# A cross-attention block: projection products 1 and 7 in quarters, softmax inverses read back from DRAM, the second score tile lowered on VectorE

## The chip, the cores and the metric

One NeuronCore of a Trainium2 chip runs the whole program. The metric is device time in microseconds for one execution. Five engines run their own instruction lists side by side, each in order: TensorE (matmuls, with weight loads shown apart), VectorE, ScalarE, GpSimd, and SyncE, which here only issues DMAs. Semaphores join them.

## The reference

```python
xq  = _ada_ln(x_q,  t_vec, Wss_q,  bss_q)      # x: (16, 1024, 512), layer norm, scaled and shifted per batch
xkv = _ada_ln(x_kv, t_vec, Wss_kv, bss_kv)     # context: (16, 64, 512)
q   = (xq @ Wq + bq).reshape(B, Lq, nh, dh)    # 16 heads of 32
kv  = (xkv @ Wkv + bkv).reshape(B, Lkv, 2, nh, dh)
scores = jnp.einsum('bqhd,bkhd->bhqk', q, k) / jnp.sqrt(jnp.float32(dh))
attn = jax.nn.softmax(scores, axis=-1)
out  = jnp.einsum('bhqk,bkhd->bqhd', attn, v).reshape(B, Lq, H)
return x_q + (out @ Wp + bp)
```

All of it is float32. Nearly all the arithmetic lies in the two 512x512 products over 16,384 rows: the query projection and the output projection.

## The kernel before

**Tiling.** The rows are cut into NB = 32 blocks of 512, two per batch element. Keys and values of all batch elements are made on the way in and stay in SBUF. A block i then passes through these stages, each a small helper:

- `load_x` (1 MB), `q_stats` (two VectorE instructions for each of four 128-row tiles), `q_scale` (five small ScalarE and four small GpSimd operations), `hidden` (ScalarE normalises), `turn` and `move` (VectorE transposes 32x32 pieces, 16 DMAs put them in place), `scale_features` (ScalarE), `feature_sums` (GpSimd).
- `query_product(i, 1..7)`: the 512-row block and the weights are each cut into 2x2 halves, and seven products with sums around them take the place of eight. A product is four matmuls of 128x128 weights and 256 columns. Each float32 matmul shows as two records in the trace, so a product has eight. Query products 1 and 7 are cut once more by the same scheme: `feature_quarters` (GpSimd, three additions), `quarter_products` (seven matmuls of 128 columns, the first four and the last three apart), `quarter_copies` (ScalarE) and `quarter_adds` (VectorE, three additions in PSUM between the two parts). `query_out` (ScalarE) and `query_added` (VectorE) take the results out.
- `score_products(i, z)` for z = 0, 1, the two halves of 32 keys. It fills two pairs of PSUM banks, and there are just two such pairs (`ps_s`, two buffers), so the next user of a pair has to wait for all its readers. `maximum(i, z, e)` (VectorE) and `copied(i, z, e)` (ScalarE, into `s_tiles`) read them. `maxima` joins the maxima and spreads them over a tile `mb`.
- `subtract` for both z (GpSimd, 2048 elements per partition each), `weights` (exp on ScalarE), `swapped` and `again` (the first half of the weights is rearranged so that `mix` can contract over 64 rows), `total` (GpSimd adds both halves), `row_total` (VectorE sums over the keys).
- `inverse_rows`: VectorE's reciprocal, a write to DRAM, four reads of 8 KB back. `spread_rows` (VectorE transposes a broadcast of them over a whole tile `vb`). `mix(i)` uses the same two pairs of score banks; `divided(i, (e,))` multiplies them by `vb` into `ot` and so frees them.
- `row_sum` (GpSimd, four sums over halves of `ot`), `biased` and `output_seed` (ScalarE puts the bias, or a copy of the other bank, into a PSUM bank), `product(i, 1..7)` for the output projection in the same seven-product scheme, `added` (VectorE adds a bank to the residual tile), and an output DMA after `added` 3 and 4.

**Order.** Nothing is scheduled by a library: the calls at the end of the function, from line 1296 on, give every engine its list, in that order. Lines 1296 to 1757 are the way in, lines 1759 to 1875 the steady loop over i = 3 to 29, the rest the way out. A round of the loop works on several blocks at once: scores of i, statistics of i + 4, query products of n = i + 1, mixing and projection of a = i - 1 and b = i - 2. All DMAs of the loop are issued by SyncE, in order, and an issue that waits for a semaphore holds up those behind it.

**Helpers that are there, but not called.** The file holds `inner_weight_sums`, `inner_biased`, `inner_quarters`, `inner_products`, `inner_copies`, `inner_adds`, `reciprocal_rows`, `read_rows`, `q_stats_two` and `q_square_mean`; `lowered` is called for block 30 alone.

Of the kernel before, what the change touches and what calls it, by code (L numbers as in the profile page):

```python
# [20 lines left out]
def cross_attention_block(  # L21
# [1646 lines left out]
    query_product(3, 6)  # L1668
    turn(4, (3,))
    load_x(6)  # L1670
    row_total(1)
    added(0, 2)
    query_product(3, 2)
    move(4, ks=(0,))
    again(1, 0)
    inverse_rows(1)
    weight_sums()
    move(4, ks=(1,))
    move(4, ks=(2,))
    biased(0, 3)  # L1680
    maximum(2, 1, 1)
    maximum(2, 1, 0)
    maxima(2)
    product(0, 7)
    move(4, ks=(3,))
    row_sums(0, 1)
    product(0, 6)
    again(1, 1)
    hidden(5, (0,))
    subtract(2, zs=(0,))  # L1690
    added(0, 7)
    product(0, 4)
    hidden(5, (1,))
    added(0, 6)
    q_stats(6, (0,))
    query_out(3, 2)
    query_out(3, 6)
    product(0, 5)
    q_stats(6, (1,))
    q_stats(6, (2,))  # L1700
    q_stats(6, (3,))
    added(0, 5)
    feature_sums(3, nc.gpsimd, (3,))
    spread_rows(1)
    copied(2, 1, 1)
    copied(2, 1, 0)
    mix(1)
    product(0, 3)
    added(0, 4)
    subtract(2, zs=(1,))  # L1710
    weights(2, 0)
    added(0, 3)
    divided(1)
    row_sums(1, 0)
    turn(5, (0,))
    turn(5, (1,))
    turn(5, (2,))
    hidden(5, (3,))
    query_product(3, 7)
    query_out(3, 7)  # L1720
    query_product(3, 5)
    query_added(3, 5)
    weights(2, 1)
    query_product(3, 4)
    biased(1, 2)
    product(1, 1)
    scale_features(4, (2,))
    turn(5, (3,))
    load_x(7)
    added(1, 1)  # L1730
    scale_features(4, (0,))
    scale_features(4, (1,))
    scale_features(4, (3,))
    product(1, 2)
    total(2)
    feature_quarters(4, 1)
    query_product(3, 3)
    query_added(3, 4)
    swapped(2)
    added(1, 2)  # L1740
    feature_sums(4, nc.gpsimd, (0,))
    biased(1, 3)
    row_total(2)
    move(5, ks=(0,))
    row_sums(1, 1)
    query_out(3, 3)
    feature_sums(4, nc.gpsimd, (1,))
    q_scale(6)
    feature_sums(4, nc.gpsimd, (2,))
    weight_quarter_sums(7)  # L1750
# [3 lines left out]
    inverse_rows(2)  # L1754
    feature_sums(4, nc.gpsimd, (3,))
    move(5, ks=(3,))
    load_residual(2)

    for i in range(3, NB - 2):
        a, b, n, f = (i - 1, i - 2, i + 1, i + 2)  # L1760
        score_products(i, 0)
        maximum(i, 0, 0)
        quarter_products(n, 1, True)
# [26 lines left out]
        if i + 4 < NB:  # L1790
            q_stats(i + 4, (0,))
# [267 lines left out]
```

## Time and profile before

| | |
|---|---|
| median of 3 runs | 998.18 us (997.47 to 998.61) |
| the profiled execution | 996.79 us, with a span of 994.9 us |
| granted TensorE clock | 1.0 throughout |
| one round of the loop | 28.57 us |

The span runs from the first to the last instruction of the profile. Busy time counts overlapping instructions of an engine once. A line such as L1155 is that of the helper that issues the instruction, so projection products of all blocks stand under one line; the names left and right of the arrow are output and inputs. A wait is put down to the engine whose signal came last. The ends of matmuls are modelled, so their starts are what to measure with.

### The profile page before, as it was taken

What the parts mean: (1) busy time and instruction counts of PE and PEld (TensorE: products, weight loads), DVE (VectorE), ACT (ScalarE), POOL (GpSimd) and SP (SyncE); (2) the same over time, 40 slices, a digit from 0 to 9 for tenths busy, and PEclk for the clock granted to TensorE, in tenths of its full rate; (3) what the DMA queues carried; (4) which work ended last, traced back from release to release, by engine and by line L of the source; (5) the groups of instructions that cost most, each with busy time, mean ns of one, the idle gap of its engine ahead of it and who ended that gap; (6) DMA issues with size and microseconds to landing.
All of it is one profiled execution on the core that took longest, in us unless ns stands there. A gap on an engine that the chain in (4) does not pass through costs nothing.

```text
span 994.9 us, 20661 instructions
## 1 busy us (share of the span) xinstructions
PE 982.9 (99%) x7501; PEld 767.7 (77%) x7501; DVE 898.5 (90%) x1326; ACT 780.2 (78%) x1169; POOL 893.0 (90%) x695
## 2 busy tenths in 40 slices
PE   8999999999999999999999999999999999999997
PEld 7888777777777777777777778777787787777776
DVE  7687899999999999999999999999999999987995
ACT  3878868888888888888888888888888888876540
POOL 2687999999999999999999999999999999999861
PEclk9999999999999999999999999999999999999999
DMA  9765755555656555556655555565555556544323
GB/s 316 257 173 148 172 161 143 156 161 171 190 181 181 164 152 164 142 180 191 184 178 159 160 154 151 182 188 181 178 152 172 149 155 182 148 135 131 116 90 108
DMA packets 114885, 165.52 MB, mean 166 GB/s; under 512 B 34872, under 2 KB 46160, under 8 KB 112864
## 3 DMA queue, kind: packets, MB, share of 16 engines
q1 hardware_dynamic: 114400, 163.67, 55.2%
q8 instruction: 60, 0.98, 0.4%
q0 software_dynamic: 384, 0.54, 0.2%
q14 instruction: 41, 0.34, 0.1%
HBM read 79.21 MB, written 34.60 MB: 114 GB/s over the span
## 4 chain that ended last, share of the span: by engine, by line
PE 94%; POOL 1%; DMA 1%; SPq 1%; DVE 1%; issue 1%; DVEq 0%; ACT 0%; POOLq 0%
PE pp L1155 37%; PE pq L551 29%; PE pq L622 10%; PE ps L755 7%; PE po L1002 6%; PE pk_A L551 1%; PE pv_B L551 1%; PE pk_B L551 1%; PE pv_A L551 1%; DMA w_k_sb<-in_L_xcond_Wkv_dram 1%; PE pp_0b L1155 1%; POOL sum L902 0%; SPq L166 0%; SPq L143 0%; DVE m L772 0%
## 5 line engine op out<-in xcount | busy, mean ns | idle before, releaser
L814 POOL TENSOR_TENSOR s<-s,mb 128x2048 f32<-128x2048 f32 x63 | 286.1, 4563 | 16.5 <-DVE mb L801 9.2
L1155 PE MATMUL pp<-w_p_sb,ot 128*128 128x256 f32 x756 | 178.9, 380 | 0.2 <-DVE ot L981 0.2
L772 DVE TRANSPOSE_TENSOR_REDUCE m<-ps 128x32 f32<-128x1024 f32 x128 | 152.3, 1226 | 10.0 <-PE ps L755 9.7
L781 ACT COPY s<-ps 128x1024 f32<-128x1024 f32 x126 | 127.4, 1013 | 41.8 <-PE ps L755 36.9
L1155 PEld LDWEIGHTS pp<-w_p_sb,ot 128*128 128x128 f32 x756 | 141.2, 190 | 21.9 <-issue 1.9
L662 ACT ACTIVATE qt<-pq,bias_t 128x256 f32<-128x256 f32 x256 | 107.5, 474 | 52.9 <-PE pq L622 27.8
L902 POOL TENSOR_TENSOR sum<-s,p 128x2048 f32<-128x2048 f32 x30 | 136.4, 4547 | 1.6 <-ACT p L836 1.6
L1288 DVE TENSOR_TENSOR r<-pp,r 128x512 f32<-128x512 f32 x188 | 123.6, 669 | 14.2 <-ACT xt L459 6.8
L551 PE MATMUL pq<-xt,w_q_sums 128*128 128x256 f32 x512 | 123.8, 385 | 0.0
L1155 PE MATMUL pp<-WT,ot 128*128 128x256 f32 x508 | 122.0, 383 | 0.0
L551 PEld LDWEIGHTS pq<-xt,w_q_sums 128*128 128x128 f32 x512 | 95.2, 190 | 34.3 <-issue 22.6
L1155 PE MATMUL pp<-WT,s 128*128 128x256 f32 x504 | 119.6, 380 | 0.7 <-DVE r L1288 0.5
L861 ACT ACTIVATE s<-s 32x2048 f32<-32x2048 f32 x60 | 114.6, 1910 | 1.5
L1155 PEld LDWEIGHTS pp<-WT,ot 128*128 128x128 f32 x508 | 94.2, 190 | 17.8 <-issue 3.0
L1155 PEld LDWEIGHTS pp<-WT,s 128*128 128x128 f32 x504 | 91.5, 191 | 11.9 <-DVE r L1288 1.4
L344 ACT ACTIVATE x<-x,rstdq 128x512 f32<-128x512 f32 x128 | 94.8, 807 | 1.0 <-POOL rstdq L305 0.9
L459 ACT ACTIVATE xt<-xt,ss_q 128x512 f32<-128x512 f32 x124 | 93.9, 807 | 0.5 <-DMA xt<-ht 0.3
L981 DVE TENSOR_TENSOR ot<-po,vb 128x1024 f32<-128x1024 f32 x64 | 75.5, 1219 | 18.8 <-PE po L1002 17.4
L287 DVE BATCH_NORM_STATS2 bs<-x 128x6 f32<-128x512 f32 x128 | 85.3, 666 | 0.0
L510 POOL TENSOR_TENSOR xt_sums<-xt 128x512 f32<-128x512 f32 x64 | 81.2, 1268 | 1.4 <-ACT xt L459 0.9
L374 DVE STREAM_TRANSPOSE ht<-x 128x512 f32<-128x512 f32 x124 | 77.7, 679 | 4.3 <-ACT x L344 2.2
L907 DVE TRANSPOSE_TENSOR_REDUCE lt<-sum 128x64 f32<-128x2048 f32 x31 | 71.6, 2310 | 6.2 <-POOL sum L902 3.9
(221 smaller groups left out, 1957.6 us busy)
## 6 DMA issues: line engine op xcount, KB each, us to landing
x<-in_x_dram SPq DMA_DIRECT2D x32, 1024.0 KB, 5.4
r<-in_x_dram SPq DMA_DIRECT2D x32, 1024.0 KB, 5.7
out_dram<-r SPq DMA_DIRECT2D x62, 512.0 KB, 5.0
xt<-ht SPq DMA_DIRECT2D x488, 64.0 KB, 2.0
p<-s SPq DMA_DIRECT2D x60, 256.0 KB, 3.8
wss_kv<-in_L_xcond_Wss_kv_dram SPq DMA_DIRECT2D x4, 512.0 KB, 7.2
wss_q<-in_L_xcond_Wss_q_dram SPq DMA_DIRECT2D x4, 512.0 KB, 10.5
vr<-ltd SPq DMA_DIRECT2D x128, 8.0 KB, 1.8
```

Source lines behind the costliest of these rows:

```text
L344: nc.scalar.activation(dst, src, AF.Identity, bias=rstd[:, 1, j : j + 1], scale=rstd[:, 0, j : j + 1])
L459: nc.scalar.activation(xt[:, :, c, :], xt[:, :, c, :], AF.Identity, scale=ss["q"][:, c, b : b + 1], bias=ss["q"][:, NC + c, b : b + 1],)
L551: nc.tensor.matmul(out_, lhsT=lhsT, rhs=rhs, start=new and m == 0 and c == 0, stop=c == HC - 1, skip_group_check=True,)
L622: nc.tensor.matmul(qa["q", k][:, q * P : (q + 1) * P], lhsT=lhsT, rhs=rhs, start=first and q == 0, stop=True, skip_group_check=True,)
L662: nc.scalar.activation(dst, src, AF.Identity, bias=bq_t[:, o : o + 1])
L772: nc.vector.tensor_reduce(m_tiles[i][:, z, 2 * e : 2 * e + 2, :], s_banks[i, z][e].rearrange("p r (j a) -> p r j a", a=32), AX.X, ALU.max, ...
L781: nc.scalar.copy(s_tiles[i, z][:, 2 * e : 2 * e + 2, :], s_banks[i, z][e])
L814: eng.tensor_tensor(s_tiles[i, z], s_tiles[i, z], mb_tiles[i], ALU.subtract)
L861: nc.scalar.activation(s_tiles[i, 0][at + 32 : at + 64], raw_tiles[i][at : at + 32], AF.Exp, scale=SCALE)
L902: nc.gpsimd.tensor_tensor(t, s_tiles[i, 0], s_tiles[i, 1], ALU.add)
L1155: nc.tensor.matmul(to, lhsT=rows[:, c, t * P : (t + 1) * P], rhs=cols[:, c, :], start=n == 2 and (i, 2) not in seeded and t == 0 and c == ...
L1288: nc.vector.tensor_add(r, a, r)
```

## The change

Five things change. First, for blocks 2 to 28, projection products 1 and 7 are made in quarters, as query products 1 and 7 already are: `product(i, 1)` and `product(i, 7)` with their `biased` give way to `inner_biased` (two half-size copies into the bank), `inner_quarters` (three GpSimd additions), `inner_products` in two parts, `inner_copies` (ScalarE) and `inner_adds` (three VectorE additions):

```python
def inner_quarters(i, v, eng=nc.gpsimd):
    ...
    tt(t[:, 0:2], x[:, 1, 0:2, :], x[:, 0:2, 0, :], ALU.subtract)
    tt(t[:, 2], x[:, 1, 1, :], t[:, 0], ALU.subtract)
    tt(t[:, 3], x[:, 0, 1, :], t[:, 2], ALU.subtract)
def inner_adds(i, v):
    a, t, tt = acc[acc_bank(i, v)], inner_tiles[i, v], nc.vector.tensor_tensor
    both_ = a[:, P : 3 * P].rearrange("p (k n) -> p k n", k=2)
    tt(t[:, 2], a[:, 3 * P :], t[:, 0], ALU.add)
    tt(both_, both_, t[:, 2:3].to_broadcast([P, 2, P]), ALU.add)
    tt(a[:, 3 * P :], a[:, P : 2 * P], t[:, 1], ALU.add)
```

The weight sums for it are made on the way in by `inner_weight_sums(1)` and `(7)` on GpSimd. They overwrite a part of the weights and of a bias, which the new `inner_restored` puts back for blocks 29 to 31.

Second, from block 2 to block 30 the inverses are spread by DMA: `reciprocal_rows` makes the reciprocal, transposes it (64 elements per partition) and writes it to DRAM, and `read_rows` reads it back in four DMAs that each broadcast rows over 32 partitions of `vb`. `spread_rows` goes there.

```python
def reciprocal_rows(i):
    ...
    nc.vector.reciprocal(flat, flat)
    nc.vector.transpose(v.rearrange("p k a -> p (k a)"), flat)
    nc.sync.dma_start(d.rearrange("k x a -> x k a"), v)
def read_rows(i, rs=range(HPC)):
    ...
        src = src[r % 2 : r % 2 + 1].to_broadcast([32, NC, TB])
        nc.sync.dma_start(vb_tiles[i][32 * r : 32 * r + 32], src)
```

Third, for blocks 3 to 30, the second score tile isn't copied out by ScalarE and then lowered by GpSimd. `lowered(i, e)` on VectorE subtracts the maxima straight from the PSUM banks into the SBUF tile, in two instructions of 1024 elements per partition.

Fourth, for one of the four tiles of a block, from block 7 on, the statistics are made by `q_stats_two` on ScalarE (two passes of 512 elements with accumulators) and `q_square_mean` on GpSimd.

Fifth, the loop body is rotated and its order is new. The first part of a round now finishes the query products of i, mixes b and begins its projection; the part after `score_products(i, 0)` is the later one. The order of the last part of the way in and of the way out is new too. The banks of the projection are swapped for block 30, where they were swapped for 29 and 31.

```diff
-        return (2 if n in (1, 6, 5, 3) else 3) - (2 if i in (NB - 3, NB - 1) else 0)
+        return (2 if n in (1, 6, 5, 3) else 3) - (2 if i == NB - 2 else 0)
...
-            z_halves.append(bank(f"pp_{i}_0", 0))
+            z_halves.append(bank(f"pp_{i}_0", 2))
...
+    def inner_restored(v):
+        tt = nc.gpsimd.tensor_tensor
+        tt(inner_weight(v, 1, 0), inner_weight(v, 0, 0), inner_weight(v, 1, 0), ALU.subtract)
+        if v == 7:
+            tt(b_diff[:, P:], b_diff[:, P:], b_diff[:, :P], ALU.add)
...
```

The order of a round after, for i = 4 to 28 and with the conditions on i left out. Calls separated by semicolons stand on lines of their own in the file:

```python
quarter_adds(i, 7); scale_features(n, (0,)); scale_features(n, (1,)); product(i - 3, 3); mix(b)
subtract(a, zs=(0,)); scale_features(n, (3,)); quarter_products(i, 7, False); query_product(i, 5)
added(i - 3, 3); turn(f, (1,)); divided(b, (0,)); feature_quarters(n, 1); added(i - 3, 4)
weights(a, 0); inner_biased(b, 1); query_out(i, 7); inner_quarters(b, 1); divided(b, (1,))
inner_products(b, 1, True); turn(f, (2,)); weights(a, 1); query_added(i, 5); turn(f, (3,))
row_sum(b, 0); query_product(i, 4); load_x(i + 4); inner_copies(b, 1); inner_adds(b, 1)
q_stats_two(i + 3, (0,)); total(a); query_product(i, 3); query_added(i, 4); move(f, ks=(0,))
query_out(i, 3); q_stats(i + 3, (1,)); inner_products(b, 1, False); score_products(i, 0)
row_sum(b, 2); scale_features(n, (2,)); quarter_products(n, 1, True); q_stats(i + 3, (2,))
output_seed(b); q_stats(i + 3, (3,)); swapped(a); copied(i, 0, 1); quarter_copies(n, 1)
row_sum(b, 1); product(b, 2); maximum(i, 0, 0); maximum(i, 0, 1); q_square_mean(i + 3, range(1))
inner_quarters(b, 7); quarter_adds(n, 1); product(b, 6); added(b, 2); copied(i, 0, 0)
row_total(a); move(f, ks=(1,)); feature_sums(n, nc.gpsimd, (0,)); feature_sums(n, nc.gpsimd, (1,))
quarter_products(n, 1, False); q_scale(i + 3); inner_biased(b, 7); inner_products(b, 7, True)
query_seed(n); feature_sums(n, nc.gpsimd, (2,)); inner_copies(b, 7); move(f, ks=(2,)); again(a, 0)
hidden(i + 3, (3,)); score_products(i, 1); query_product(n, 2); reciprocal_rows(a); query_out(n, 2)
hidden(i + 3, (0,)); row_sum(b, 3); load_residual(a); move(f, ks=(3,)); added(b, 6)
inner_adds(b, 7); maximum(i, 1, 1); again(a, 1); hidden(i + 3, (2,)); inner_products(b, 7, False)
product(b, 5); query_product(n, 6); feature_quarters(n, 7); maximum(i, 1, 0); read_rows(a, (0, 1))
quarter_products(n, 7, True); added(b, 7); product(b, 4); query_out(n, 6); maxima(i); added(b, 5)
read_rows(a, (2, 3)); quarter_copies(n, 7); lowered(i, 1); hidden(i + 3, (1,))
feature_sums(n, nc.gpsimd, (3,)); lowered(i, 0); turn(i + 3, (0,))
```

More of the change, by code (lines that the diff above doesn't have):

```diff
@@ L1688, in cross_attention_block @@
+    inverse_rows(1)
+    again(1, 0)
+    maximum(2, 1, 1)
+    query_out(3, 2)
+    feature_sums(3, nc.gpsimd, (2,))
+    maxima(2)
+    product(0, 6)
+    added(0, 6)
+    hidden(5, (2,))
+    hidden(5, (3,))
+    scale_features(4, (0,))
+    added(0, 7)
+    scale_features(4, (1,))
+    query_product(3, 7)
+    product(0, 5)
+    added(0, 5)
     again(1, 1)
+    load_x(6)
+    copied(2, 1, 0)
+    copied(2, 1, 1)
+    query_product(3, 6)
     hidden(5, (0,))
+    query_out(3, 6)
+    product(0, 4)
@@ L1724, in cross_attention_block @@
+    product(1, 1)
+    added(0, 4)
     query_product(3, 4)
-    biased(1, 2)
-    product(1, 1)
     scale_features(4, (2,))
+    feature_sums(4, nc.gpsimd, (0,))
     turn(5, (3,))
+    query_product(3, 3)
     load_x(7)
-    added(1, 1)
[L1731 to L1739, printed above, removed]
+    query_added(3, 4)
+    product(1, 2)
+    inner_weight_sums(1)
@@ new lines, in cross_attention_block @@
+        if i >= 4:
+            move(f, ks=(3,))
+        added(b, 6)
+        if i >= 4:
+            inner_adds(b, 7)
+        maximum(i, 1, 1)
+        again(a, 1)
+        if i < NB - 3:
+            hidden(i + 3, (2,))
+        if i >= 4:
+            inner_products(b, 7, False)
+        product(b, 5)
+        query_product(n, 6)
+        feature_quarters(n, 7)
+        maximum(i, 1, 0)
+        if i >= 4:
+            read_rows(a, (0, 1))
+        quarter_products(n, 7, True)
+        added(b, 7)
@@ L1869, in cross_attention_block @@
-        load_residual(i)
-        row_sum(a, 3)
-        feature_sums(f, nc.gpsimd, (2,))
-        feature_sums(f, nc.gpsimd, (3,))
-        product(a, 7)
-        if i == NB - 3:
-            load_residual(NB - 1)
-    y, z = (NB - 2, NB - 1)
+    y, z = (NB - 2, NB - 1)
+    scale_features(31, (0,))
+    product(27, 3)
+    scale_features(31, (1,))
+    added(27, 4)
+    mix(28)
+    quarter_adds(30, 7)
+    added(27, 3)
+    divided(28, (0,))
+    divided(28, (1,))
+    subtract(29, zs=(0,))
@@ new lines, in cross_attention_block @@
+    quarter_products(30, 7, False)
+    scale_features(31, (3,))
+    inner_biased(28, 1)
+    weights(29, 0)
+    feature_quarters(31, 1)
+    query_out(30, 7)
+    query_product(30, 5)
+    query_added(30, 5)
+    weights(29, 1)
+    load_residual(NB - 1)
+    load_residual(29)
+    inner_quarters(28, 1)
+    inner_products(28, 1, True)
+    query_product(30, 4)
+    query_product(30, 3)
+    inner_copies(28, 1)
+    scale_features(31, (2,))
+    inner_adds(28, 1)
+    row_sum(28, 0)
+    total(29)
@@ L1877, in cross_attention_block @@
+    query_added(30, 4)
+    swapped(29)
+    inner_products(28, 1, False)
+    row_sum(28, 2)
+    row_sum(28, 1)
+    feature_sums(31, nc.gpsimd, (0,))
+    query_out(30, 3)
     score_products(y, 0)
+    inner_quarters(28, 7)
+    output_seed(28)
     maximum(y, 0, 0)
@@ L1920, in cross_attention_block @@
-    query_added(z, 5)
+    added(28, 2)
+    quarter_products(z, 1, False)
+    inner_biased(28, 7)
+    query_seed(z)
+    feature_sums(31, nc.gpsimd, (1,))
+    row_total(29)
+    inner_products(28, 7, True)
+    added(y - 2, 6)
+    score_products(y, 1)
+    inner_copies(28, 7)
+    inner_adds(28, 7)
+    again(y - 1, 0)
+    feature_sums(31, nc.gpsimd, (2,))
+    reciprocal_rows(29)
+    maximum(y, 1, 0)
+    query_product(z, 2)
+    query_out(z, 2)
+    inner_products(28, 7, False)
+    maximum(y, 1, 1)
@@ new lines, in cross_attention_block @@
+    query_product(z, 6)
+    maxima(y)
+    feature_quarters(z, 7)
+    quarter_products(z, 7, True)
+    again(y - 1, 1)
+    product(y - 2, 5)
+    row_sum(28, 3)
+    added(y - 2, 7)
+    query_out(z, 6)
+    quarter_copies(z, 7)
+    lowered(y, 0)
+    read_rows(29, (0, 1))
+    lowered(y, 1)
+    query_product(z, 5)
+    added(y - 2, 5)
+    read_rows(29, (2, 3))
+    quarter_adds(z, 7)
+    weights(y, 1)
+    product(y - 2, 4)
+    subtract(y, zs=(0,))
+    added(y - 2, 4)
+    inner_restored(1)
@@ L1953, in cross_attention_block @@
[L1953 to L1977 removed]
+    subtract(z, zs=(1,))
```

537 lines of the change are left out of this document (277 added, 260 removed).

## The prediction

> **What bounds the kernel now.** I read the page's first two parts and its chain, then busy time by round of the steady loop, then forms of instruction, waits, and timelines of one round.
>
> ```profile
> span 994.9 us, 20661 instructions
> PE 982.9 (99%) x7501; PEld 767.7 (77%) x7501; DVE 898.5 (90%) x1326; ACT 780.2 (78%) x1169; POOL 893.0 (90%) x695
> PE 94%; POOL 1%; DMA 1%; SPq 1%; DVE 1%; issue 1%; DVEq 0%; ACT 0%; POOLq 0%
> ```
>
> TensorE is 99% busy and 94% of the chain, but a busy share hides how near the others are. Two table answers of busy time by stretch say it: one round of the loop, with the mean of ten such rounds, then three stretches outside it (stretch, its length; busy time and instructions of TensorE, its weight loads, VectorE, ScalarE, GpSimd; granted clock, DMA share, GB/s).
>
> ```profile
> 500.00:528.57 28.57, 28.57 (x222) 22.22 (x221) 27.03 (x40) 24.07 (x36) 27.56 (x23) 1.00 0.59 174
> sum 285.70, PE 285.70 PEld 222.31 DVE 270.16 ACT 240.62 POOL 275.42; mean PE 28.57 PEld 22.23 DVE 27.02 ACT 24.06 POOL 27.54
> ...
> 120.00:160.00 40.00, 39.72 (x292) 30.38 (x291) 36.74 (x48) 30.44 (x42) 39.05 (x34) 1.00 0.53 151
> 940.00:960.00 20.00, 18.24 (x187) 12.15 (x186) 18.42 (x19) 8.54 (x11) 12.94 (x7) 1.00 0.31 109
> 980.00:994.90 14.90, 9.38 (x44) 7.86 (x42) 6.47 (x13) 0.00 (x0) 1.68 (x2) 0.98 0.39 142
> ```
>
> A round takes 28.57 us, all of it TensorE. VectorE has 1.54 us left, GpSimd 1.0, ScalarE 4.5. So TensorE work that goes is worth its time only until VectorE is full, and the change moves work onto VectorE. That is the whole question.
>
> **TensorE: what is saved.** The query products 1 and 7 already have the form that projection products 1 and 7 get. A stretch of TensorE's timeline shows both forms side by side (start, length, what; starts count, since lengths overlap).
>
> ```profile
> 500.93 1.89 PE L551 MATMUL pq<-xt_sums,w_q_sums 128*128 128x256 f32 x8
> 502.66 0.38 PE L622 MATMUL pq<-xt_sums,w_q_sums 128*128 128x128 f32 x2
> 502.88 0.83 PE L622 MATMUL pq<-t_quarters,w_p_sb 128*128 128x128 f32 x6
> 503.55 0.81 PE L1155 MATMUL pp<-w_p_sb,ot 128*128 128x256 f32 x3
> ```
>
> A whole product is 8 records in 502.66 − 500.93 = 1.73 us, 216 ns each. The first four small products are 8 records in 503.55 − 502.66 = 0.89 us, 111 ns each. Seven of them are 14 records, 1.56 us. A product saves 0.17 us, a round 0.33, and TensorE needs 28.24. 27 blocks (2 to 28) change, so the whole could give 27 × 0.33 = 8.9 us.
>
> The Trainium skill ("TensorE: Matmul & The Clock Gate", Back-to-back issue gap) speaks against this: in a stream of weight loads and matmuls it gives about 81 ns for 128 columns, against 56 for a lone one, since the load counts too. By that ratio (an estimate from the page's figures) a small record would take 111 × 81 / 56 = 161 ns and a product 2.25 us, 0.5 more than now, some 28 us over 27 blocks. The rows above are such a stream, and show 111: the trace does not agree, and the sum goes without that rule.
>
> **VectorE: what is added.** Forms with their mean, two waits, and two stretches of its timeline:
>
> ```profile
> L957 DVE STREAM_TRANSPOSE vb<-vr 128x2048 f32<-128x2048 f32 x31 | 71.3, 2301 | 0.7 <-DMA vr<-ltd 0.7
> L818 DVE TENSOR_TENSOR s<-ps,mb 128x1024 f32<-128x1024 f32 x2 | 2.4, 1220 | 0.1
> L287 DVE BATCH_NORM_STATS2 bs<-x 128x6 f32<-128x512 f32 x128 | 85.3, 666 | 0.0
> L288 DVE BATCH_NORM_AGGREGATE mvq<-bs 128x2 f32<-128x6 f32 x128 | 23.3, 182 | 4.4
> L374 DVE STREAM_TRANSPOSE ht<-x 128x512 f32<-128x512 f32 x124 | 77.7, 679 | 4.3 <-ACT x L344 2.2 <-ACT qt L662 1.0 <-DMA xt<-ht 0.8
> ...
> DVE ot L981 <- PE po L1002: 17.4, 26, 1.1
> DVE m L772 <- PE ps L755: 9.7, 28, 1.0
> ...
> 523.87 0.25 DVE L639 TENSOR_TENSOR t_quarters<-pq,t_quarters 128x128 f32<-128x128 f32 x1
> 524.16 0.43 DVE L640 TENSOR_TENSOR pq<-pq,t_quarters 128x256 f32<-128x256 f32 x1
> 524.63 0.30 DVE L641 TENSOR_TENSOR pq<-pq,t_quarters 128x128 f32<-128x128 f32 x1
> 524.84 0.68 DVE L1288 TENSOR_TENSOR r<-pp,r 128x512 f32<-128x512 f32 x1
> 525.48 2.38 DVE L772 TRANSPOSE_TENSOR_REDUCE m<-ps 128x32 f32<-128x1024 f32 x2
> ```
>
> Independent neighbours overlap by 0.09 and 0.04 here (524.63 + 0.30 against 524.84, 524.84 + 0.68 against 525.48), about 0.07; dependent ones leave 0.04 (524.16 + 0.43 against 524.63). Per round:
> - `lowered` twice, 1.22 each less 0.07: +2.30.
> - `inner_adds` twice. The trace has no such line, but `quarter_adds` has the same three forms: 524.84 − 523.87 = 0.97 each, +1.94.
> - the small transpose in `reciprocal_rows`, 64 elements. No row shows one. Between the smallest VectorE row (0.18) and the 512-element transpose (0.68); the line through 512 (0.68) and 2048 (2.30) gives 0.20, and I take that.
> - `spread_rows` gone: 2.30 less 0.07, −2.23.
> - one tile's statistics to ScalarE: 0.67 + 0.18 less an overlap, −0.81.
>
> Sum +1.40. What VectorE needs now is 27.0 to 27.5: busy 27.02, while of the 1.54 idle about 17.4/26 + 9.7/28 = 1.0 are waits for TensorE, which end when VectorE never catches up; each that ends gives back an overlap of 0.07, so I take the low end. After: 28.4 to 28.9, taken 28.4. **VectorE takes over as the bound**, 0.16 above TensorE's 28.24, and 0.17 below the old round.
>
> **What covers the rest.** GpSimd and ScalarE, by these forms; the DMAs with KB and median landing; one issue on SyncE's timeline:
>
> ```profile
> L814 POOL TENSOR_TENSOR s<-s,mb 128x2048 f32<-128x2048 f32 x63 | 286.1, 4563 | 16.5 <-DVE mb L801 9.2 <-ACT qt L662 7.2
> L598 POOL TENSOR_TENSOR t_quarters<-xt 128x256 f32<-128x256 f32 x28 | 20.5, 732 | 0.0
> L599 POOL TENSOR_TENSOR t_quarters<-xt,t_quarters 128x128 f32<-128x128 f32 x28 | 12.9, 460 | 2.2
> L781 ACT COPY s<-ps 128x1024 f32<-128x1024 f32 x126 | 127.4, 1013 | 41.8 <-PE ps L755 36.9 <-DVE m L772 3.9
> L633 ACT COPY t_quarters<-pq 128x256 f32<-128x256 f32 x56 | 21.0, 374 | 2.7 <-PE pq L622 1.8
> L1099 ACT COPY pp<-b_diff 128x512 f32<-128x512 f32 x32 | 18.8, 589 | 42.8 <-DVE r L1288 42.8
> L344 ACT ACTIVATE x<-x,rstdq 128x512 f32<-128x512 f32 x128 | 94.8, 807 | 1.0 <-POOL rstdq L305 0.9
> ...
> x<-in_x_dram SPq DMA_DIRECT2D x32, 1024.0 KB, 5.4
> p<-s SPq DMA_DIRECT2D x60, 256.0 KB, 3.8
> ltd<-lt SPq DMA_DIRECT2D x32, 32.0 KB, 1.7
> ...
> 499.52 0.59 SPq L399 DMA_DIRECT2D xt<-ht  x1
> ```
>
> GpSimd loses one subtraction (4.56) and gains two `inner_quarters` of 0.73 + 0.46 + 0.46 with gaps near 0.08 (3.6 together) and a tiny multiplication (0.2): about 26.8 of 28.4. ScalarE loses two copies (−2.03) and two bias copies (−1.18); it gains four half-size ones and two `inner_copies` (six at 0.374, +2.24) and two passes of `q_stats_two` at 0.59 to 0.81 each, with an accumulator write that no row shows (at most another small 0.3 each): +0.2 to +1.2 on 24.06. Its 4.5 us idle hide that; without them it would be added whole.
>
> The inverse now goes out and comes back as four broadcasts of 256 KB. On SyncE's queue they stand behind the write (1.7), the residual load and four moves. Between the reciprocal and the next `divided` VectorE's list holds four large additions and two transposes (0.6 each), six small additions (1.94), two maxima (2.4), the spread of the maximum (2.3, the form of `spread_rows`, and 0.3) and the two `lowered` (2.3): 12.8 us. Write 1.7, ten issues at 0.59 and a landing of 3.8 (5.4, the 1 MB load, at worst) make 11.4 to 13.0. I cost it at nothing; at worst `divided` comes 0.2 late, and then both pairs of score banks. Behind the two reads, which wait for the write to land, SyncE's queue holds the next round's outputs, its load of x and its moves. Those moves feed `scale_features` a round later, and the moves of this round are issued ahead of the reads, so nothing near waits for them. The DMA share rises from 0.59 by about 1 MB in 5, to some 0.7.
>
> All other steps are moved, not changed: product 3 and the additions of products 3 and 4 cross into the next round with their two output DMAs, `swapped` goes behind `total` by a score product, the residual load ahead of the reads, the statistics of block i+3 stand where those of i+4 stood. Each keeps its engine and length, so the sums hold; what a new order can cost is waits, below. Projection bank numbers shift for block 30 in place of 29 and 31, on the way out.
>
> The way in gains about 5 us on GpSimd (`inner_weight_sums`, ten small operations near 0.46), between 120 and 160 us, where it is busy 39.05 of 40; round 3 gives a subtraction back. Between 0 and +5; I take +0.7. The way out has 1.8 + 5.5 us of idle TensorE: a new order could win or lose 2 either way; I take 0, with the 0.33 of block 28.
>
> **Sum.** Rounds 4 to 29: 26 × (28.57 − 28.40) = 4.4; + 0.3 − 0.7 = 4.0 faster. The profiled execution took 996.79 (span 994.9 and 1.9 around it), so 992.8; the median of the three runs, 998.18, is 1.4 above it, so **994.2**.
>
> **The rivals.**
>
> *TensorE keeps the lead.* If VectorE's order closes up better than I sum (28.2), the full 8.9 comes: 989.3. For it: four more instructions that overlap. Against: a VectorE without a single wait.
>
> *A draw.* The saving is eaten by VectorE at 28.5 to 28.6, or in the way in: 996.2 to 1000.2, center 998.2. For it: the upper half of my bounds begins right there.
>
> *Slower: the ring through the score banks.* Before, ScalarE's copies freed the second pair of score banks. Now `lowered`, last but one on VectorE's list, frees it; `mix` needs that pair and `divided` needs `mix`.
>
> ```profile
> 507.45 0.39 PE L622 MATMUL pq<-t_quarters,w_q_sums 128*128 128x128 f32 x2
> 507.76 1.09 PE L1002 MATMUL po<-s,V_A 64*32 64x512 f32 x16
> 508.65 1.06 PE L1002 MATMUL po<-p,V_A 64*32 64x512 f32 x16
> 509.64 2.00 PE L551 MATMUL pq<-xt,w_q_sums 128*128 128x256 f32 x8
> 509.80 2.36 DVE L981 TENSOR_TENSOR ot<-po,vb 128x1024 f32<-128x1024 f32 x2 [0.65 <-PE po L1002]
> ```
>
> `mix` takes 509.64 − 507.76 = 1.88, and `divided` starts 0.16 later: 2.04. VectorE has two transposes (0.61 each), three small additions (0.97) and one large (0.60) between, 2.8. So TensorE may come to `mix` at most 0.7 us late, with `product(i-3, 3)`, 1.73 us, queued ahead of it. If it comes later, VectorE waits, and behind that wait stand its whole list and, through the inner products, TensorE. It decides from 0.17 us of VectorE wait a round. Half of today's 1.0 gives 28.9, 26 × 0.33 = 8.6 more, 1006.
>
> **How the numbers follow.** Forecast (faster than 996.2) 0.42; TensorE leads 0.11; draw 0.21; slower 0.26. Own range of the forecast: 991 to 996. The range for 8 in 10 leaves out the best of the second and the worse half of the last: 987.5 to 1004. Under 0.2% (2 us) a measurement of this kernel can't be told from no change. Faster 0.53, within 0.21, slower 0.26.
>
> **What would show it.** In a round after: TensorE with 0.1 to 0.3 us idle where it had none, VectorE over 28 of some 28.4; `inner_products` at 111 ns a record; `divided` with waits for `mix` under 0.2 us a round (the ring, if 0.5); no wait for the broadcasts. Wrong if the round exceeds 28.57, if the way in puts off the first round by several us, or if the broadcasts land late.

## The result, and the profile after

The changed kernel takes 1030.57 us (median of four runs, 1026.54 to 1033.39), the kernel before 998.3 beside it: a ratio of 1.0322, with an interval from 1.0284 to 1.0359. It is 32 us slower, where 4 us faster was forecast. The profiled execution took 1033.39 us, with a span of 1031.6.

The first and fourth parts of the page after: span, busy time, and the chain that ended last, by engine.

```profile
span 1031.6 us, 22024 instructions
PE 998.7 (97%) x7825; PEld 779.8 (76%) x7825; DVE 922.3 (89%) x1492; ACT 796.4 (77%) x1323; POOL 869.7 (84%) x869
DVE 40%; DMA 31%; PE 21%; issue 3%; POOL 3%; SPq 2%; ACT 1%; DVEq 0%; POOLq 0%
```

Before, TensorE held 94% of the chain and DMAs 1%. Now DMAs hold 31%, and VectorE, which starts when they land, 40%. The starts of the score products divide the span (us, read from the trace; score 4 is the first of block 4):

| | before | after | load behind the reads | way in rearranged |
|---|---|---|---|---|
| start of the first score product | 59.35 | 61.84 | 59.80 | 59.53 |
| start of score 4 | 177.92 | 182.41 | 179.86 | 178.30 |
| score 4 to score 29, 25 rounds | 713.11 | 740.38 | 711.28 | 709.65 |
| one round | 28.52 | 29.62 | 28.45 | 28.39 |
| score 29 to the end | 103.87 | 108.82 | 107.56 | 106.95 |

(The last two columns are runs told below.) Of the 36.7 us that the span grew, 27.3 are in the loop, 4.9 behind it, 2.0 in the way in and 2.5 ahead of the first score product, where both kernels hold the same instructions: there the granted clock was 0.83 from 20 to 30 us in this execution, 1.00 before, which is 1.7 of the 2.5. The 28.57 us that stands for a round of before ahead of the prediction is the width of the stretches that were asked for; by the starts of the score products it is 28.52. What a round waits for stands in the waits of after, and the landing times in its DMA issues (KB, median us to landing):

```profile
DVE ot L981 <- DMA vb<-ltd: 26.0, 22, 2.5
DVE ot L981 <- PE po L1002: 0.6, 1, 0.6
ACT xt L459 <- DMA xt<-ht: 20.7, 15, 2.9
ACT xt L459 <- DMA vb<-ltd: 17.4, 10, 2.7
...
r<-in_x_dram SPq DMA_DIRECT2D x32, 1024.0 KB, 6.5
xt<-ht SPq DMA_DIRECT2D x488, 64.0 KB, 3.3
vb<-ltd SPq DMA_DIRECT2D x116, 256.0 KB, 6.4
```

`divided` (L981) waits for the broadcasts in 22 rounds, 26.0 / 22 = 1.2 us each. That is the growth of a round. The broadcasts land in 6.4 us, where 3.8 was taken and 5.4 was the worst allowed for; the moves take 3.3 for 2.0, and `scale_features` (L459) waits for them. It reads only what the moves bring, though ten of its waits are put down to the broadcasts. One round on SyncE's timeline, then on VectorE's, and the chain through it:

```profile
517.36 0.53 SPq L938 DMA_DIRECT2D ltd<-vr  x1
517.93 0.49 SPq L126 DMA_DIRECT2D r<-in_x_dram  x1
518.48 2.41 SPq L399 DMA_DIRECT2D xt<-ht  x4
521.29 3.84 SPq L948 DMA_DIRECT2D vb<-ltd  x4
...
515.83 0.55 DVE L936 RECIPROCAL lt<-lt 128x64 f32<-128x64 f32 x1
...
528.57 0.70 DVE L374 STREAM_TRANSPOSE ht<-x 128x512 f32<-128x512 f32 x1
530.30 1.23 DVE L981 TENSOR_TENSOR ot<-po,vb 128x1024 f32<-128x1024 f32 x1 [1.03 <-DMA vb<-ltd]
...
517.93 6.88 DMA r<-in_x_dram
524.83 5.35 DMA vb<-ltd
```

VectorE's list from the reciprocal's end (516.38) to where `divided` could start (529.27) is 12.9 us long; the prediction counted 12.8. But the last broadcast lands at 524.83 + 5.35 = 530.18, 13.8 after the reciprocal, where 11.4 to 13.0 was worked out. The chain runs through the 1 MB residual load, issued between the write and the reads.

### The profile page after: what moved, and what is told of

It is laid out like the page before. It is cut to its first block, busy times and chain, and to the rows that moved or that the text cites. A ratio compares the mean times of both kernels' runs of the same rounds, so it can differ in the third digit from the quotient of the medians.

```text
span 1031.6 us, 22024 instructions
## 1 busy us (share of the span) xinstructions
PE 998.7 (97%) x7825; PEld 779.8 (76%) x7825; DVE 922.3 (89%) x1492; ACT 796.4 (77%) x1323; POOL 869.7 (84%) x869
## 4 chain that ended last, share of the span: by engine, by line
DVE 40%; DMA 31%; PE 21%; issue 3%; POOL 3%; SPq 2%; ACT 1%; DVEq 0%; POOLq 0%
DMA r<-in_x_dram 15%; DMA vb<-ltd 14%; PE pq L551 7%; DVE m L772 6%; DVE lt L907 5%; DVE ot L981 5%; DVE bs L287 4%; DVE r L1295 4%; PE pp L1155 3%; DVE ht L374 3%; DVE qt L669 3%; PE ps L755 2%; DVE pp L1271 2%; PE pk_A L551 1%; POOL s L814 1%
## 5 line engine op out<-in xcount | busy, mean ns | idle before, releaser
L814 POOL TENSOR_TENSOR s<-s,mb 128x2048 f32<-128x2048 f32 x36 | 164.1, 4563 | 23.7 <-DVE mb L801 21.5
L1155 PE MATMUL pp<-w_p_sb,ot 128*128 128x256 f32 x540 | 128.0, 380 | 1.8 <-ACT pp L1108 0.7
L459 ACT ACTIVATE xt<-xt,ss_q 128x512 f32<-128x512 f32 x124 | 94.6, 810 | 38.8 <-DMA xt<-ht 20.7
L551 PE MATMUL pq<-xt,w_q_sums 128*128 128x256 f32 x512 | 121.1, 379 | 0.0
L1155 PEld LDWEIGHTS pp<-w_p_sb,ot 128*128 128x128 f32 x540 | 98.0, 190 | 16.3 <-issue 2.7
L981 DVE TENSOR_TENSOR ot<-po,vb 128x1024 f32<-128x1024 f32 x64 | 77.7, 1220 | 31.7 <-DMA vb<-ltd 26.0
L344 ACT ACTIVATE x<-x,rstdq 128x512 f32<-128x512 f32 x128 | 103.7, 818 | 2.1 <-POOL rstdq L305 1.0
L1155 PEld LDWEIGHTS pp<-WT,s 128*128 128x128 f32 x504 | 93.5, 190 | 12.8 <-DVE r L1295 0.8
L374 DVE STREAM_TRANSPOSE ht<-x 128x512 f32<-128x512 f32 x124 | 85.9, 697 | 10.5 <-DMA xt<-ht 5.4
L781 ACT COPY s<-ps 128x1024 f32<-128x1024 f32 x72 | 72.8, 1014 | 12.0 <-PE ps L755 6.1
L551 PEld LDWEIGHTS pq<-xt,w_q_sb 128*128 128x128 f32 x288 | 52.0, 189 | 32.6 <-ACT seventh L1264 22.6
L836 ACT ACTIVATE s<-s 128x2048 f32<-128x2048 f32 x34 | 64.8, 1908 | 14.6 <-POOL s L814 11.1
L801 DVE STREAM_TRANSPOSE mb<-m 128x2048 f32<-128x2048 f32 x32 | 74.0, 2311 | 1.2
```

The lines of the kernel that those rows point to most:

```text
L344: nc.scalar.activation(dst, src, AF.Identity, bias=rstd[:, 1, j : j + 1], scale=rstd[:, 0, j : j + 1])
L374: nc.vector.transpose(ht_tiles[i][:, :, :, t, :].rearrange("p k c b -> p c k b"), x_tiles[i][:, t, :].rearrange("p (c k b) -> p c k b", c= ...
L551: nc.tensor.matmul(out_, lhsT=lhsT, rhs=rhs, start=new and m == 0 and c == 0, stop=c == HC - 1, skip_group_check=True,)
L814: eng.tensor_tensor(s_tiles[i, z], s_tiles[i, z], mb_tiles[i], ALU.subtract)
L981: nc.vector.tensor_tensor(ot[:, cs, :], po[e], vb[:, cs, :], ALU.mult)
L1155: nc.tensor.matmul(to, lhsT=rows[:, c, t * P : (t + 1) * P], rhs=cols[:, c, :], start=n == 2 and (i, 2) not in seeded and t == 0 and c == ...
```

## The experiments

**Where the reads lose their time.** In after, the fourth read is issued late, since its issue waits until the residual load has landed, eight DMAs earlier (26 such waits, 50.6 us together): the four issues above take 3.84 us. The first run issues one move ahead of the load, so that the fourth read is seven DMAs behind it, and no longer waits. The second puts the load behind the reads.

```diff
 # one move ahead
+    move(f, ks=(3,), gs=(0,))
     load_residual(a)
-    move(f, ks=(3,))
+    move(f, ks=(3,), gs=(1, 2, 3))
 # load behind the reads
-    load_residual(a)
     move(f, ks=(3,))
 ...
     read_rows(a, (2, 3))
+    load_residual(a)
```

> The changed kernel, but one of the four moves that stood behind the residual load is issued ahead of it; the load itself starts about 0.6 us later, and beside the reads as before. Theory Q (queue): in the changed kernel's trace the fourth read of a round is issued 1.9 us after the third, when the residual load has landed, which was issued exactly eight DMAs earlier; with one move between, that wait goes, the last read is issued 0.5 us after the third and lands about 1.5 us sooner, the 1.0 us of VectorE's wait for it goes, and a round falls from 29.6 to 28.6 us: about 1005. Theory B (bandwidth: the reads land late because 1 MB of residual is moved beside their 1 MB): the round stays at 29.4 to 29.6, about 1029. Theory V (VectorE is full at 28.3 us busy and its gaps make the rest): 29.6, about 1030.

> The changed kernel with the residual load issued behind the four reads of the round. Takes away the queue's wait and the traffic beside the reads at once. Q: as with one move ahead, 28.6 a round, about 1005. B: 28.5, about 1003, with the reads landing in about 4 us in place of 6.4, and clearly below the run with one move ahead. V: 29.6, about 1030.

One move ahead: 1030.43 us (1028.45 to 1031.86), ratio 1.033 (1.0313 to 1.0346). The four reads are issued in 1.76 us, yet they land no sooner (DMA issues and a wait of this run):

```profile
vb<-ltd SPq DMA_DIRECT2D x116, 256.0 KB, 7.2
DVE ot L981 <- DMA vb<-ltd: 25.3, 23, 2.3
```

The issue queue falls as a cause: only the next DMA, an output, now waits for the load (26 waits, 52.4 us). Load behind the reads: 1000.5 us (999.58 to 1001.99), ratio 1.0028 (1.0016 to 1.0041). The same rows, and a round of its busy time by stretches:

```profile
r<-in_x_dram SPq DMA_DIRECT2D x32, 1024.0 KB, 7.9
vb<-ltd SPq DMA_DIRECT2D x116, 256.0 KB, 4.8
DVE ot L981 <- DMA vb<-ltd: 2.6, 1, 2.6
...
456.88:485.32 28.44, 28.44 (x240) 22.53 (x233) 27.90 (x46) 24.58 (x42) 26.45 (x28) 1.00 0.70 198
```

The reads land in 4.8 us, the load pays (7.9) and nobody waits for it, and the round is 28.44. So 30 of the 32 us came from the place of one load. A third run asks whether one queue served in order makes the reads late, or the sharing of the DMA engines: the load keeps its place, but ScalarE issues it.

```diff
-    load_residual(a)
+    load_residual(a, nc.scalar)
```

> Edit: the changed kernel, with the residual load of the loop at its place in the list, but issued by ScalarE on its own queue in place of SyncE's. Nothing is left out. It asks why the load beside them makes the reads late. Theory O (one queue in order: the reads' packets stand behind the megabyte in each engine's ring, as one queue serves them in turn): with the load on another queue the reads land in about 4.8 us as with the load behind them, the round is 28.44 to 28.5, the time 1000 to 1003. Theory S (the 16 engines share their time whatever the queue): reads and load still run side by side, landing 6 us or more, round 29.3 to 29.7, time 1024 to 1033. In between (landing near 5.5, round 28.7 to 29.2) both have a part.

```profile
vb<-ltd SPq DMA_DIRECT2D x116, 256.0 KB, 7.3
r<-in_x_dram ACTq DMA_DIRECT2D x26, 1024.0 KB, 6.2
DVE ot L981 <- DMA vb<-ltd: 28.7, 24, 2.7
```

1030.98 us in one execution, as slow as on one queue. The order within a queue falls too. What is left, by exclusion, is that load and reads share the DMA engines, whichever queue they come from.

**Whether VectorE and TensorE were sized right.** One run brings the old spread by VectorE back into the loop (`inverse_rows`, `spread_rows`), and the four broadcasts go. Another, with the load behind the reads, goes back to whole products 1 and 7 (the weight sums, `inner_restored` and all steps of the small products go with them).

```diff
-    reciprocal_rows(a) ... read_rows(a, (0, 1)) ... read_rows(a, (2, 3))
+    inverse_rows(a)    ...                          spread_rows(a)
```

> The changed kernel with the inverses of blocks 3 to 28 spread by VectorE's transpose again, the residual load where the change put it. VectorE gets 2.2 us more and loses a small transpose: 28.3 + 2.0 = 30.3 us busy in a round. Q and B: VectorE becomes the bound, a round of 30.4 to 30.8, about 1050. If the round should fall below 29.6, the reads cost more than VectorE's transpose, and VectorE was not near its end (against V and against my sum).

```diff
-    inner_biased(b, 1) ... inner_products(b, 1, True) ... inner_products(b, 1, False)
+    biased(b, 2)       ... product(b, 1)
     # the same for product 7
```

> The run with the residual load behind the reads, and projection products 1 and 7 of all blocks whole again (the weight sums and what puts the weights back go too). TensorE then needs 28.5 us a round as before the change, VectorE 26.4. Q and B: 28.5 to 28.6 a round, bound by TensorE; the difference to the run with the residual behind is what the small products bring. If VectorE is the bound there at 28.6 or more, this run is as fast or faster. V: 28.5, since VectorE is relieved.

With the spread back, 1055.64 us and a round of 30.58, in quiet rounds 30.14 to 30.30. The price worked out, 2.23 less the 0.20 of the small transpose, put on the 28.4 predicted for VectorE makes 30.4. Whole products: 1026.33 us, a round of 29.44, where 28.5 to 28.6 was expected. The order was written for products in two parts; without the second part nothing stands between query product 3 and the scores, and the waits show it:

```profile
DVE m L772 <- PE ps L755: 41.1, 58, 3.1
PE ps L755 <- ACT qt L662: 16.4, 29, 0.6
```

So that run doesn't price the small products by themselves.

**Why the round is 28.44 and not 28.24.** With the load behind the reads TensorE has no gap in a round. But a busy stretch hides a wait. The timeline of all engines at the first score product of a round (start, length, engine, line):

```profile
463.90 0.84 ACT L662 ACTIVATE qt<-pq,bias_t 128x256 f32<-128x256 f32 x2 [0.74 <-PE pq L551]
464.46 1.45 PE L755 MATMUL ps<-qt,K_A 32*32 32x512 f32 x32
464.79 0.21 PEld L755 LDWEIGHTS ps<-qt,K_A 32*32 32x32 f32 x24 [0.18 <-ACT qt L662]
465.85 0.49 PE L622 MATMUL pq<-xt,w_q_sb 128*128 128x128 f32 x2
```

From its start to the next product it takes 465.85 - 464.46 = 1.39 us, the second score product of a round 1.07. Eight weight loads go in, those of the first of four column groups, then 24 wait for the second half of `query_out`. That is 0.31 of the 0.33 that a round saves; without it TensorE would need 28.13 where before took 28.52. Only the 0.67 us second part of the small product now stands between query product 3 and the scores, where before had a whole projection product of 1.73. The next runs try to fill the hole: by taking the column groups in another order, then by rearranging the way in as well, then by halves of query products 4 and 3.

```diff
 # scores turned (blocks 4 to 29, first score product)
-    for c in range(NC):
+    for c in (2, 3, 0, 1):
 # way in, on top of it
-    copied(2, 1, 0)  copied(2, 1, 1)  ...  subtract(2, zs=(1,))
+    lowered(2, 0)    lowered(2, 1)
+    query_out(3, 3)  score_products(3, 0)    # ahead of biased(1, 3), product(1, 7)
+    load_residual(2)                         # behind read_rows(2, (2, 3))
```

> Edit: the residual load behind the reads, as in the run before, and the first score product takes its four column groups in the order 2, 3, 0, 1 in place of 0, 1, 2, 3, in blocks 4 to 29. Nothing is left out. Open after the last runs: the round was 28.44 us and TensorE without a gap in it, where the prediction needed 28.24. Theory H (a hidden hole): the small products do save 0.33 us a round, but the first score product starts on group 0 and then stands 0.3 us inside what counts as one busy stretch, since the second half of product 3's query_out (columns 0 and 1) ends after it began; groups 2 and 3 had their last addition 0.9 us earlier. Turned round, the hole is filled with groups 2 and 3, and the round falls to what the next engine allows: TensorE 28.13, VectorE 28.2 to 28.3 by the run that gave it 2.3 us more. So 28.25 (28.13 to 28.35), 26 rounds x 0.19 = 5 less than 1000.5: 995.5 (992.5 to 998). Theory F (TensorE is full at 28.44, the score product simply takes that long): round 28.44, time 1000.5 +- 1. A third way, VectorE already bounds at 28.4: round 28.40 to 28.44, with TensorE showing a gap elsewhere.

> Edit: the run above, and three moves in the way in: block 2's second score tile lowered by VectorE from the score banks (lowered, twice) in place of two copies by ScalarE and one subtraction of 4.6 us by GpSimd; query_out(3,3) and the first score product of block 3 ahead of biased(1,3) and product(1,7); the residual load of block 2 behind its reads. Nothing is left out. Theory W (the way in lost its 2 us to GpSimd, full from 120 to 165 us, and to waits that this order exposes): TensorE's waits there, 1.50 for the bias copy, 0.71 for a row sum of GpSimd and 0.65 for the late division, go, and the loop starts 1.5 to 2.9 us earlier: 995.5 - 2 = 993.5 (992.5 to 995) if the run above gives 995.5, in any case 1.5 to 2.9 below it. Theory N (the way in is set by something else, a DMA or VectorE): the same time as the run above within 0.7.

Scores turned: 999.54 us, ratio 1.0017 (1.0008 to 1.0026), most rounds 28.38. The hole went only from 0.31 to 0.25 us (321.42 - 320.10 = 1.32):

```profile
320.10 1.39 PE L755 MATMUL ps<-qt,K_A 32*32 32x512 f32 x32
321.42 0.49 PE L622 MATMUL pq<-xt,w_q_sb 128*128 128x128 f32 x2
```

The four column groups run side by side: the group that waits is now the last, its loads go in 0.33 us after the start, and the product still takes 0.99 from there. Way in rearranged: 998.1 us, ratio 1.0008 (0.9999 to 1.0017), no difference that can be measured from before. A stretch of the way in with the load behind the reads, then with this rearrangement, and a round of the latter:

```profile
120.00:160.00 40.00, 37.79 (x281) 28.57 (x280) 33.22 (x45) 26.78 (x42) 38.87 (x39) 1.00 0.52 144
...
120.00:160.00 40.00, 37.78 (x281) 28.56 (x280) 35.20 (x47) 25.42 (x39) 34.52 (x38) 1.00 0.51 143
...
456.80:485.20 28.40, 28.40 (x234) 22.62 (x233) 27.91 (x46) 24.66 (x42) 26.48 (x28) 1.00 0.72 205
```

GpSimd falls from 38.87 to 34.52 of 40 us, yet TensorE's idle 2.2 stays there: the wait moved to a later row sum of GpSimd (1.7). Score 4 comes 1.6 us earlier, the lower end of what was expected. A further run puts sums of `inner_weight_sums(1)` into an idle stretch of GpSimd and the row sums ahead of the rest:

> Edit: the run with the way in rearranged (998.1, round 28.38), and on GpSimd in the way in three of the four sums of inner_weight_sums(1) with its bias into the 4.35 us in which GpSimd stood idle ahead of row_sums(1,0), and row_sums(1,1) ahead of the rest. Nothing is left out. Theory W (what is left of the way in's loss is GpSimd's list): TensorE's wait of 1.72 us for a row sum of GpSimd, the longest that is left there, falls to nothing, and the loop starts 1 to 1.7 us earlier: 996.4 to 997.1. Theory V adds: the round stays at 28.38, since nothing of it is changed, so that the whole lands level with the kernel before or at most 0.1% under it. Theory N (the wait only moves to the next row sum or to a bias copy): 997.8 to 998.4.

999.9 us, ratio 1.0017. The wait moved on, to VectorE's additions for the query's small product:

```profile
PE pq L622 <- DVE pq L641: 1.9, 1, 1.9
```

**What holds the round at 28.38.** In the run with the way in rearranged, no two VectorE instructions of the loop lie more than 0.04 us apart, over ten rounds in the trace. It is as full as it can be, at 28.38; the prediction had 28.40. Is it the bound? Six more runs. The first takes query products 4 and 3 by halves, so that the first half of `query_out` can start earlier; the second gives ScalarE one more statistic of VectorE's; the third takes out the waits that the first had made.

```diff
 # halves; with the statistics of a second tile on ScalarE: q_stats_two(i + 3, (3,))
-    query_product(i, 4)  query_product(i, 3)  query_out(i, 3)
+    query_product(i, 4, (0,))  query_product(i, 3, (0,))  query_out(i, 3, (0,))
+    query_product(i, 4, (1,))  query_product(i, 3, (1,))  query_out(i, 3, (1,))
 # halves apart: query_product(i, 4, (0,)) moves ahead of inner_products(b, 1, True)
```

> Edit: the run with the way in rearranged, the score product's column groups in their old order 0 to 3, and query products 4 and 3 of the loop taken by halves in the order 4 (first half), 3 (first), 4 (second), 3 (second), with query_out(i,3) following each half of product 3, and one statistic ahead of the addition of product 4. Nothing is left out. The turned groups brought the round from 28.44 to 28.38 only: the groups of one score product run side by side, so the last group's wait still stands in it (0.25 of 0.31 us), and VectorE shows no wait at all. Two theories of what now holds the round at 28.38. Theory T (TensorE, through the wait of the score product for ScalarE's query_out): now the first half of query_out runs 0.9 us earlier and the second ends before the score product begins, the hole goes, and the round falls towards 28.13: 28.15 to 28.25, time 998.1 - 26 x 0.18 = 993.5 (992 to 995). Theory V (VectorE, as the prediction had it, 28.4 with its list full): the round stays at 28.36 to 28.42, TensorE shows gaps of some 0.25 us a round elsewhere, time 997 to 999.

> Edit: the run above, and in the loop the statistics of a second tile of x taken by ScalarE (q_stats_two for tile 3), which takes 0.67 + 0.18 less an overlap = 0.81 us a round off VectorE and puts 1.6 us on ScalarE, busy 24.65 of 28.38. Nothing is left out. Theory V (VectorE is the bound at 28.38): VectorE's list needs 27.6, and the round falls to TensorE's 28.13 to 28.25: 992 to 995.5, while the run above stays at 28.38. Theory T (TensorE is the bound): the same round as the run above, or a longer one where ScalarE's list, which then has 2 us left, delays a copy that TensorE waits for (28.5 or more).

> Edit: as the run with query products 4 and 3 by halves, but without the waits that its order made: the first half of product 4 stands ahead of the first part of the small product 1 (and query_out(i,7) ahead of the bias copies, so that the bank is free), the addition of product 5 one transpose earlier on VectorE, and ScalarE's first pass of the statistics between the two halves of query_out, the second behind them. The order on TensorE is 5, 4 (first half), small 1 (first part), 3 (first), 4 (second), 3 (second), small 1 (second part), scores. Nothing is left out. The run before it had the score product at its full 1.07 us, but 0.67, 0.10 and 0.10 us of new waits in the halves: round 29.01, of which 28.13 is TensorE's own work. Theory T (TensorE's waits alone hold the round): without them it falls to 28.13 to 28.28; 998.1 - 26 x 0.15 = 994 (992 to 996). Theory V (VectorE's list is full at 28.38 whatever TensorE does): the round stays at 28.36 to 28.42 and the time at 997 to 999. If the halves still wait on ScalarE's query_out, which frees their bank, the round is over 28.45.

Halves: 1013.0 us, ratio 1.0147, round 29.01. With two tiles on ScalarE: 1015.65, ratio 1.0172, round 29.11; VectorE stands 1.4 us a round there, so that run tells nothing of its list as a bound. The hole at the scores is gone, but the first half of product 3 now waits for VectorE's addition of product 5, whose bank it needs, and VectorE waits for the late scores:

```profile
437.82 1.13 PE L551 MATMUL pq<-xt,w_q_sums 128*128 128x256 f32 x4 [0.29 <-DVE qt L669]
442.64 2.38 DVE L772 TRANSPOSE_TENSOR_REDUCE m<-ps 128x32 f32<-128x1024 f32 x2 [0.23 <-PE ps L755]
```

Halves apart: 1000.92 us, ratio 1.0037, round 28.52. The scores take 1.07 to 1.17 there. But a new hole stands ahead of the first part of small product 7 (its TensorE timeline, then ScalarE's):

```profile
441.86 0.39 PE L624 MATMUL pq<-t_quarters,w_q_sb 128*128 128x128 f32 x2
442.31 0.46 PE L1255 MATMUL pp<-WT,ot 128*128 128x128 f32 x2
...
441.83 0.38 ACT L1208 COPY pp<-zero 128x256 f32<-128x256 f32 x1
```

Two small records are 0.22 us, here 0.45: the bias copy ends 0.1 before the product starts. The last three runs take one statistic off VectorE altogether (a tile is normalised with its neighbour's, so a part of the computation is left out), open that hole, and do both.

```diff
 # one statistic less
-    q_stats(i + 3, (3,))
+    nc.vector.bn_aggr(q_mv[i + 3][:, 3, :], last_bs[0])
 # ring opened
-    quarter_adds(n, 1)  product(b, 6)  added(b, 2)  ...  q_scale(i + 3)  inner_biased(b, 7)
+    added(b, 2)  quarter_adds(n, 1)  product(b, 6)  ...  inner_biased(b, 7)  q_scale(i + 3)
```

> Edit: the run of the halves without their waits (1000.9, round 28.52), less one VectorE instruction a round: the statistics of tile 3 of each x block in the loop are not taken; tile 3 is normalised with tile 2's, so a part of the computation is left out (0.67 us of VectorE less about 0.07 of overlap; no other engine has less to do). In the last runs VectorE went through its list without a gap over 0.04 us, at 28.38 in one order and 28.52 in another, while TensorE's own work was 28.13. Theory V (VectorE's list is what holds the round): it falls by 0.6 to 27.9, TensorE takes over, and the round is 28.13 to 28.28: 26 x 0.3 = 7 less, 993 to 995.5. Theory T (something on TensorE's side, a bank or a copy, holds it, and VectorE is dense by chance): the round stays at 28.45 to 28.55, VectorE shows gaps of 0.6 us a round, time 1000 to 1002.

> Edit: the run of the halves without their waits (1000.9, round 28.52), with added(b,2) ahead of quarter_adds(n,1) on VectorE and inner_biased(b,7) ahead of q_scale(i+3) on ScalarE. Nothing is left out. In that run TensorE stood 0.39 us ahead of the first part of small product 7: its bias copies on ScalarE ended 0.1 before it, they stood behind the five small operations of q_scale, and waited for VectorE's added(b,2), which stood behind three small additions. Theory V (VectorE's list of 28.38 to 28.42 holds the round): the round falls to 28.38 to 28.42 and no further, 997.5 to 999. Theory T (only such waits hold it): it falls by 0.3 to 28.15 to 28.25, 992 to 995. If the wait only moves to the second part of the query's small product, behind the same additions, 28.45 to 28.55.

> Edit: the run above, less the statistics of tile 3 in the loop (tile 3 is normalised with tile 2's, so a part of the computation is left out): 0.6 us a round less for VectorE, nothing else. Theory V: VectorE's list is 27.8, TensorE takes over, the round is 28.13 to 28.28, 0.15 to 0.25 under the run above. Theory T: the same round as the run above within 0.03.

One statistic less: 1001.42 us, and the round stays 28.52, with gaps of 0.7 us a round on VectorE. Ring opened: 1003.41, ratio 1.0055, round 28.60; opened with one statistic less: 1003.23, round 28.60. The wait moved to just ahead of it, to the second part of the query's small product, behind the same VectorE additions (TensorE's timeline; eight records that take 1.73 us elsewhere take 444.56 - 442.53 = 2.03):

```profile
442.53 1.89 PE L1157 MATMUL pp<-WT,s 128*128 128x256 f32 x8
444.56 0.68 PE L624 MATMUL pq<-xt,w_q_sb 128*128 128x128 f32 x4
```

So in these two orders the length of VectorE's list doesn't hold the round: 0.6 us less of it changes nothing. VectorE already waits in them with the statistic, which the expectations overlook: in most rounds 0.12 us ahead of the second maximum, too short for the lists of waits. A second maximum with the statistic (its score product starts at 464.32), then both maxima without it (score product at 437.54):

```profile
467.10 1.25 DVE L774 TRANSPOSE_TENSOR_REDUCE m<-ps 128x32 f32<-128x1024 f32 x1
...
438.84 1.25 DVE L777 TRANSPOSE_TENSOR_REDUCE m<-ps 128x32 f32<-128x1024 f32 x1 [0.29 <-PE ps L760]
440.32 1.25 DVE L777 TRANSPOSE_TENSOR_REDUCE m<-ps 128x32 f32<-128x1024 f32 x1 [0.24 <-ACT s L786]
```

Either way the second maximum starts 2.78 us after the score product, right behind ScalarE's copy of the scores, which ends at 2.75. The second half of `query_out` waits 0.64 for query product 3, and from there to the end of that copy ScalarE doesn't pause. So a ring holds these rounds: from query product 3 through ScalarE's list, VectorE's second maximum and the additions behind it to the next small product.

In the order of 28.38 no work was taken off VectorE. There its list without a pause and TensorE's 28.13 with the 0.25 of hole end at the same number. The hole doesn't come from VectorE: ScalarE stands idle until product 3 is done (the run with the way in rearranged):

```profile
461.65 0.84 ACT L662 ACTIVATE qt<-pq,bias_t 128x256 f32<-128x256 f32 x2 [0.82 <-PE pq L551]
```

So less work on VectorE alone would leave TensorE at 28.38, by this trace; no run shows it, and what both together would give stays open. No version beat the kernel before.

## Why the prediction was wrong

- **The step that failed** is the cost of the reads: "I cost it at nothing; at worst `divided` comes 0.2 late", from "a landing of 3.8 (5.4, the 1 MB load, at worst)". VectorE's list (12.8, measured 12.9) was counted right. The last read was issued 8.4 after the reciprocal, where 7.6 was counted (1.7 + 5.9), but without that delay the reads landed no sooner. The landing was taken from other DMAs in other company. Four broadcasts of 256 KB beside a megabyte land in 6.4 us, 4.8 without it. `divided` came 1.2 us late, not 0.2. The move of the load was seen ("the residual load ahead of the reads") and dismissed with "Each keeps its engine and length". That alone is worth 30 us.
- **TensorE's saving** was sized right and didn't arrive. The small products issue at 111 ns a record in the trace after, as forecast (TensorE's timeline: four records from 514.79 to 515.24), so the estimate from the Trainium skill ("TensorE: Matmul & The Clock Gate", Back-to-back issue gap), by which they would be slower than whole ones, was rightly set aside: no run here shows the 161 ns worked out from its figures. But 0.31 of the 0.33 us a round goes into the score product's wait for `query_out`: the whole product that used to cover that wait had become a part of 0.67 us.

```profile
514.79 0.39 PE L1253 MATMUL pp<-b_p_sb,seventh 128*128 128x128 f32 x2
515.01 0.39 PE L1253 MATMUL pp<-WT,seventh 128*128 128x128 f32 x2
515.24 0.39 PE L1253 MATMUL pp<-b_p_sb,seventh 128*128 128x128 f32 x2
```

- **VectorE at 28.4** is what was measured without the late reads, 28.38 and gapless. That it "takes over as the bound" isn't shown: at 28.38 TensorE with its hole ends at the same number, and in the two orders in which work was taken off VectorE it already waited.
- **GpSimd and ScalarE**: 26.8 predicted, 26.5 measured; ScalarE 24.3 to 25.3 predicted, 24.6 to 24.7 measured with the reads in time.
- **The way in** cost 5.5 us (0.4 of it ahead of the first score product), not 0.7. With the load behind the reads score 4 starts 1.9 late, and by then 126 projection records are issued, before it was 136: fourteen whole products and a small one in place of seventeen, 3.6 us of TensorE's work less. The bound of +5 was just passed. The way out: 3.7 longer with 2.9 us more work in it (31 products, three of them small, for 29), so 0.7 lost, within the 2 allowed.
- **The sum without the reads.** The prediction's gain of 0.17 us a round starts from 28.57, and before takes 28.52: 25 rounds could gain 3.0 us by its own 28.40, not 4.2, and with the load behind the reads they gained 1.8 (713.11 to 711.28), 2.4 less than counted. The way in cost 4.8 more than taken. Outside the 25 rounds the forecast had 0.5 of gain (a 26th round and block 28); there 0.7 less work and the 0.7 lost on the way out cancel. From the 992.8 forecast for the profiled execution these three lead to 1000.5, and 1000.5 was measured. So there would have been no gain even with the reads in time.
- **The rivals.** No run came near the 28.2 of *TensorE keeps the lead*; the shortest steady round was 28.38. *A draw* is where the first runs with the reads in time landed (998.1 to 1000.5), but with a part of the loss in the hole at the scores, which it didn't name. The ring through the score banks fell: `divided` waits for `mix` once in after, for 0.6 us. (In five rounds its wait is put down to a TensorE product behind `mix`; `mix` had ended 0.3 us before those waits began.) It had the right sign by the wrong mechanism. What would have shown the failure was named ("or if the broadcasts land late").

## What to carry to other kernels

Here a transfer was priced by what else was on the DMA engines in the time it was under way (4.8 us or 6.4 to 7.3), whichever queue issued it: where a transfer that somebody waits for is given more bytes, move every large load that nobody waits for behind it. Work taken off a full engine is worth its time only if what it covered (here ScalarE's `query_out`) has another cover; look for the next wait inside a busy stretch, by the starts of its records.

## What the runs showed of the hardware

- In this program an issue waits for the DMA eight issues earlier: the fourth read was issued 1.9 us after the third, since the load hadn't landed. With one move ahead of the load the wait passed to the output behind the reads, the four issues took 1.76 us instead of 3.84, and the time didn't change.
- Reads of 256 KB land in 4.8 us with the megabyte behind them, in 6.4 to 7.3 beside it, on the same queue or on another.
- A score product of four column groups takes 1.07 us when all its operands are there, and 1.39 when the operand of one group, the second, comes 0.3 late. With that group last it takes 1.32. The profile shows both as one busy stretch.
